# Weighted values and second expert layers on four 32-column TensorE tiles, with other shares for the chains

## Chip, cores and metric

The kernel runs on one core of a Trainium2 chip. The metric is the device time in microseconds of one execution; the time before is the median of three runs.

## What is computed

One layer of a vision transformer over 16 images, each cut into 1024 patches of 768 numbers. Cut to what matters:

```python
h = patches @ W.T + b                            # 1024 tokens of 256
q, k, v = split(layernorm(h) @ w_qkv)            # 8 heads of 32
k = sum over f = 1..256 of a[f]*sin(f*k) + b[f]*cos(f*k)
attn = softmax(q @ k.T * scale)                  # 1024 x 1024 for each head
h = h + (attn @ v) @ w_out + b_out
n = layernorm(h)
shared = relu(relu(n @ sW1) @ sW2) @ sW3
expert[e] = relu(relu(n @ eW1[e]) @ eW2[e]) @ eW3[e]     # 4 experts, 256-128-64-256
h = h + shared + sum over the best 2 of 4 experts, weighted by their gates
```

All arithmetic is in float32, some matmuls in its float32r form.

## The kernel before

The work is laid out in 130 *rounds* (`rd`). A round holds the transform of keys for half a pair of heads and the attention of one *attention unit* `att`: a pair of heads against 512 queries. There are 128 units (4 pairs, 2 blocks of queries, 16 images), and attention runs two rounds behind the transform.

In the **transform**, integer angles are loaded from DRAM as tiles `w` (L898), or spread from `src` into `f` (L938). GpSimd multiplies them by a frequency (L953) and ScalarE takes sines (L963). `mix(g)` multiplies by coefficients into a PSUM tile `kan` (L987): 64 rows by 32 columns, eight tiles of the array at once. VectorE multiplies `kan` by the fast sines (L1001), and `add_up(q)` sums the products over the waves into `red` (L1020): 128 rows by 32 columns, four tiles at once. These are the sums over waves.

In **attention**, `score(att, kc)` forms 128 keys by 512 queries for both heads of the pair on the full array (`sT`, L1085); `exponential` takes exp on ScalarE into `es` (L1100, three buffers). `weigh(att, kc)` multiplies `es` by the values and accumulates over the eight blocks `kc` into one PSUM tile `av` (L1117). The tile `v` holds, for each pair, 32 columns of values of the first head, 32 of ones, and 32 of values of the second. Two matmuls of 64 columns each therefore give values and denominator of head 0, then denominator and values of head 1:

```python
for s in range(2):
    nc.tensor.matmul(
        out=acc[0][ts(s, 64), :],
        lhsT=v[:, kc, p % NPAIR, ds(HD * s, 64)],
        rhs=es[:, ts(s, 512)], ...
```

`normalize(att)` then takes reciprocals (L1143), multiplies into `aT` (L1150), and adds a check (L1162), on VectorE.

All the rest is **chains**, four generators that yield pieces of work: chain 0 makes keys, queries and values, chain 1 projections (`proj`), gates and networks (`s1p`, `e1p`, `s2p`, `e2p`, `e3p`, `wb`, `wT`), chain 2 the rest of the gate weights, and chain 3 tokens (`tok`) and first norms (`lnT`). In `networks`, `second_of_experts` does the second layer of two experts in one PSUM tile `e2p`, again with two matmuls of 64 columns.

The order on every engine is written out by a **planner** before the kernel is built. The fixed steps of PE, ACT and the others lie in queues by `put`; `run` lays for PE either the next fixed step or a piece of a chain. It keeps a clock per engine and adds `SWITCH` when a step's tiling (`TILINGS`, for the kinds `mix`, `av`, `red`) differs from that of the last. A fixed step in the tiling that PE is in is preferred to a piece that would change it. `PACES` gives for each chain a share: for each unit of time of fixed work on PE its debt `due` grows by the share, up to a most. A chain in debt may go ahead of a fixed step. `now["stream"]` sums the columns streamed, from which the cost of a piece follows. SP's queue issues the loads and stores; it also takes its place in this plan.

The gate's matmuls (L727) are 128 rows by 32 columns too and carry the tiling of `red`.

Of the kernel before, what the change touches and what calls it, by code (L numbers as in the profile page):

```python
# [20 lines left out]
NPAIR = 4  # L21
HD = 32
N = 1024
NT = N // P
# [29 lines left out]


LAG, LANDS, TABLE, PER_COLUMN, SWITCH, IDLE = 0.06, 2.0, 1.28, 1.0 / 600, 0.18, 0.3
PACES = ((0.155, 2), (0.44, 2), (0, 0), (0.178, 2.6))

TILINGS = {"mix": (64, 32), "av": (128, 64), "red": (128, 32)}

@with_exitstack
def plain_path(ctx: ExitStack, tc: tile.TileContext, a: dict, out: bass.AP, verdict: bass.AP):
# [9 lines left out]
    nc = tc.nc  # L72
# [58 lines left out]
    w2e = load([P, NE, 64], a["eW2"].rearrange("e p f -> p e f"), "w2e")  # L131
# [7 lines left out]
    for i in range(4):  # L139
        nc.scalar.dma_start(out=biases[ds((NE + 1) * i, NE), 0, :], in_=a["eb3"])  # L140
        nc.scalar.dma_start(
            out=biases[ds((NE + 1) * i + NE, 1), 0, :], in_=a["sb3"].unsqueeze(0)
# [54 lines left out]
    v = const.tile([P, NT, NPAIR, 96], FP, tag="v", name="v")  # L197
# [24 lines left out]
    now = {"chain": 0, "stream": 0, "table": None, "dma": 0.0, "tiling": None, "piece": None}  # L222
# [38 lines left out]
    def matmul(out, lhsT, rhs, start, stop):  # L261
        now["stream"] += max(rhs.shape[-1], P)
        nc.tensor.matmul(out=out, lhsT=lhsT, rhs=rhs, start=start, stop=stop)  # L263
# [490 lines left out]
    def networks(b, half, late=False):  # L754

        if not late:
            yield from hold("networks")
        hT = images[b]["hT", half]
        w5 = fp.tile([P, 1024], FPR, tag="f", name="w5")[0:NW5, 0:512] if late else w5_

        def room(pool, n, name):
            return late_tile(n, name) if late else pool.tile([P, n], FP, tag=name[:2], name=name)

        def hidden(lhsT, name):
            ps = side_tile(name)
            for c in range(2):
                matmul(
                    out=ps,
                    lhsT=lhsT(c),
                    rhs=hT[:, c, :],  # L770
                    start=(c == 0),
                    stop=(c == 1),
                )
            return ps

        def first_of_expert(e):
            yield GO
            ps = hidden(lambda c: w1e[:, 2 * e + c, :], "e1p")
            yield ACT, 0.6
            e1 = room(ff2, 512, "e1")  # L780
            nc.scalar.activation(e1, ps, AF.Relu, bias=b1e[:, e : e + 1])
            return e1

        def second_of_experts(u, e1):
            yield GO
            ps = side_tile("e2p")
            now["piece"] = TILINGS["av"]
            now["stream"] -= 512
            for s in range(2):
                matmul(  # L790
                    out=ps[ts(s, 64), :],
                    lhsT=w2e[:, 2 * u + s, :],
                    rhs=e1[s],
                    start=True,
                    stop=True,
                )
            yield ACT, 0.6
            t = room(ff2, 512, "e2")
            nc.scalar.activation(t, ps, AF.Relu, bias=b2e[:, u : u + 1])  # L799
            return t  # L800

        def weigh_experts(u, t):
            yield GO
            wb = side_tile("wb")
            now["stream"] -= 300
            matmul(out=wb, lhsT=sel[:, u, :], rhs=w5, start=True, stop=True)
            yield DVE, 0.63
            nc.vector.tensor_mul(t, wb, t)

        if not late:  # L810
            yield from hold("s1")
        s1 = room(ffp, 1024, "s1").rearrange("p (m n) -> p m n", m=2)
        for m in range(2):
            yield GO
            ps = hidden(lambda c, m=m: w1s[:, c, ts(m, P)], "s1p")
            yield ACT, 0.6
            nc.scalar.activation(s1[:, m, :], ps, AF.Relu, bias=b1s[:, m : m + 1])
        e1 = [(yield from first_of_expert(0))]
        yield GO
        ps = side_tile("s2p")  # L820
        for c in range(2):
            matmul(
                out=ps,
                lhsT=w2s[:, c, :],
                rhs=s1[:, c, :],
                start=(c == 0),
                stop=(c == 1),
            )
        if not late:
            locks.remove("s1")  # L830
        yield ACT, 0.6
        s2 = room(ffp, 512, "s2")
        nc.scalar.activation(s2, ps, AF.Relu, bias=b2s)
        e1.append((yield from first_of_expert(1)))
        yield lambda: "bands" not in locks
        chains[now["chain"]]["ready"] = max(ch["ready"] for ch in (chains[now["chain"]], chains[2]))
        yield GO
        ps = side_tile("wT")
        for t in range(4):
            transpose(  # L840
                ps[0:NW5, ts(t, P)],
                bands.bitcast(FP)[:, t, :, :].rearrange("p i e -> p (i e)"),
            )
        locks.remove("gates")
        yield ACT, 0.48
        nc.scalar.copy(w5, ps[0:NW5, :])
        e2 = [(yield from second_of_experts(0, e1))]
        e1 = [(yield from first_of_expert(2))]
        yield from weigh_experts(0, e2[0])
        e1.append((yield from first_of_expert(3)))  # L850
        e2.append((yield from second_of_experts(1, e1)))
        yield from weigh_experts(1, e2[1])
        h = images[b]["h", half]
        for pr in range(2):
            yield GO
            ps = side_tile("e3p").rearrange("p (t e) -> p t e", e=E)
            parts = ((s2, w3s), (e2[0], w3e[:, 0, :]), (e2[1], w3e[:, 1, :]), (w5, b3))
            for t in range(2):
                for i in range(4):
                    lhsT, rhs = parts[3 - i if t else i]  # L860
                    matmul(
                        out=ps[:, t, :],
                        lhsT=lhsT[:, ts(2 * pr + t, P)],
                        rhs=rhs,
                        start=(i == 0),
                        stop=(i == 3),
                    )
            yield DVE, 0.63
            hh = h[:, ds(2 * pr, 2), :]
            nc.vector.tensor_add(hh, ps, hh)  # L870
        nc.sync.dma_start(
            out=out[b, ts(half, 512), :].rearrange("(t p) e -> p t e", p=P), in_=h
        )
        done["written", b, half] = sent(1.6, 0.5)
        if not late:
            locks.remove("networks")
# [231 lines left out]
    def weigh(att, kc):  # L1108

        p = att // 2  # L1110

        def action():
            if kc == 0:
                acc[0] = avp.tile([P, 512], FP, tag="av", name="av")
            es = exps.pop(kc)
            for s in range(2):
                nc.tensor.matmul(  # L1117
                    out=acc[0][ts(s, 64), :],
                    lhsT=v[:, kc, p % NPAIR, ds(HD * s, 64)],
                    rhs=es[:, ts(s, 512)],  # L1120
                    start=(kc == 0),
                    stop=(kc == NT - 1),
                )

        deps = [("exp", att, kc)]
        if kc == 0:
            b, i = divmod(p, NPAIR)
            deps.append(("all values" if i == NPAIR - 1 else "values", b))
            if att > 0:
                deps.append(("norm", att - 1))  # L1130
        put(PE, "fixed", 0.86, deps, ("av", att, kc), action)
# [84 lines left out]
    for rd in range(B * RI + 2):  # L1216
        groups = range(GS * rd, min(GS * rd + GS, total))
        att = rd - 2
        attends = 0 <= att < ATT
        for g in groups[::2]:  # L1220
            first = g == groups[0]
            for i, j in ((0, 0), (0, 1), (1, 0), (1, 1), (0, 2), (1, 2)):
                sine(g + i, j, TABLE if first and i == j == 0 else 0.0)
            mix(g)
            mix(g + 1)
        if groups:
            add_up(groups[0] // 2)

        def table():
            now["table"] = AF.Exp  # L1230
            nc.scalar.activation(spare[:, 1:2], spare[:, 0:1], AF.Exp)  # L1231

        put(ACT, "fixed", TABLE + 0.2, [], ("table", rd), table)
        for n in range(0, NT + 2, 2):
            if attends and n < NT:
                for kc in (n, n + 1):
                    score(att, kc)
                    exponential(att, kc)
            if n == 2 and groups:
                add_up(groups[0] // 2 + 1)  # L1240
            if attends and n > 0:
                for kc in (n - 2, n - 1):
                    weigh(att, kc)
    with tc.manual_schedule():
        run()

# [746 lines left out]
```

## Time and profile before

| | |
|---|---|
| median of 3 runs | 4168.1 us (4166.77 to 4168.17) |
| profiled execution | 4171.0 us, span 4169.3 us, clock 0.993 |
| PE matmuls | 22753, busy 4027.4 us |
| weight loads | 22753, busy 1766.4 us |
| av (L1117) | 4096 matmuls, busy 965.1 us |
| sT (L1085) | 2048, 691.7 us |
| kan (L987) | 8192, 623.9 us |
| red (L1020) | 2048, 273.6 us |
| e2p | 256, 69.1 us |
| ACT, POOL, DVE busy | 3286.3, 3195.8, 2830.2 us |
| DMA queue of SP | 906.98 MB, 78.7% of 16 engines |

A row of a timeline gives the start of a run of like instructions, its length, the engine, the line and operation, the tiles out<-in, then for matmuls the rows and columns of the array used, the shape and the count; a bracket holds the idle time before it and what ended it. A float32 matmul of the program stands as two instructions, a float32r one (`sT`, for example) as one. "PEld" is the loading of weights, which overlaps matmuls. The ends of matmuls are modelled, so the differences between starts are the better measure.

### The profile page before, as it was taken

To read this page: it belongs to the slowest core of one execution; us is meant where nothing else is said; L and a number is where in the kernel's file an instruction comes from. 1 tells how busy PE (TensorE), PEld (TensorE's weight loads), DVE (VectorE), ACT (ScalarE), POOL (GpSimd) and SP (SyncE) were. 2 spreads that over 40 slices of the span, in tenths; PEclk is the share of its full clock that TensorE was granted. 3 is DMA by queue.
4 is the path that set the end of the run, shared out by engine and by line. 5 is a ranking of instruction groups with operands and counts; after the bars stand their busy time and mean duration, and the time that the engine had idled before them with its cause. 6 is when DMAs were issued, how large, how long until landed. Compare 5 with 4: busy or idle time off the path is not lost.

```text
span 4169.3 us, 67564 instructions
## 1 busy us (share of the span) xinstructions
PE 4027.4 (97%) x22753; PEld 1766.4 (42%) x22753; DVE 2830.2 (68%) x4172; ACT 3286.3 (79%) x3939; POOL 3195.8 (77%) x2323
## 2 busy tenths in 40 slices
PE   6889999999999999999999999999999999999998
PEld 4324344443434445344444444444444444443334
DVE  4667767677676776767767677776767767677652
ACT  2688888788787888878788888788788788888873
POOL 3988877778787887878787787888778787787850
PEclk9999999999999999999999999999999999999999
DMA  7988878888787887978878878887887978878740
GB/s 223 263 241 222 243 200 223 238 218 247 207 232 219 239 235 210 244 211 224 247 209 238 221 225 225 228 241 209 234 228 219 251 211 239 219 211 226 197 138 16
DMA packets 587478, 914.27 MB, mean 219 GB/s; under 512 B 58828, under 2 KB 177524, under 8 KB 587124
## 3 DMA queue, kind: packets, MB, share of 16 engines
q1 hardware_dynamic: 580880, 906.98, 78.7%
q8 instruction: 184, 3.01, 0.3%
q10 hardware_dynamic: 6244, 2.88, 0.3%
q14 instruction: 170, 1.39, 0.1%
HBM read 758.64 MB, written 150.99 MB: 218 GB/s over the span
## 4 chain that ended last, share of the span: by engine, by line
PE 74%; ACT 10%; DVE 6%; DMA 5%; issue 3%; SPq 2%; POOL 1%; ACTq 0%; DVEq 0%; POOLq 0%
PE av L1117 18%; PE sT L1085 11%; PE kan L987 9%; PE tok L263 6%; PE e3p L263 5%; PE red L1020 5%; PE e1p L263 5%; ACT w L963 4%; DMA w<-ud 3%; PE s1p L263 3%; PE q L263 2%; PE v L263 2%; PE proj L263 2%; DVE f L1001 2%; PE k L263 2%
## 5 line engine op out<-in xcount | busy, mean ns | idle before, releaser
L953 POOL TENSOR_TENSOR w<-w,lane 128x1024 int32<-128x1024 int32 x1024 | 1926.1, 1896 | 444.4 <-DMA w<-ud 298.6
L1100 ACT ACTIVATE es<-sT 128x1024 f32<-128x1024 f32 x1024 | 1033.0, 1022 | 550.0 <-PE av L1117 339.8
L953 POOL TENSOR_TENSOR f<-f,lane 128x1024 int32<-128x1024 int32 x512 | 971.0, 1896 | 251.2 <-DVE f L938 157.5
L963 ACT ACTIVATE w<-w 128x1024 f32<-128x1024 int32 x1024 | 1021.1, 1048 | 42.1 <-POOL w L953 39.1
L1117 PE MATMUL av<-es,v 128*64 128x512 f32 x4096 | 965.1, 602 | 1.0 <-DVE rc L1162 1.0
L1143 DVE RECIPROCAL rc<-av 128x256 f32<-128x256 f32 x256 | 434.0, 1730 | 702.6 <-PE av L1117 702.6
L1085 PE MATMUL sT<-q,k 128*128 128x512 f32 x2048 | 691.7, 449 | 42.0 <-DVE f L1001 20.2
L1001 DVE TENSOR_TENSOR f<-kan,f 128x1024 f32<-128x1024 f32 x512 | 608.5, 1218 | 159.8 <-ACT f L963 123.7
L938 DVE STREAM_SHUFFLE f<-src 128x1024 int32<-128x1024 int32 x512 | 673.0, 1353 | 0.7
L987 PE MATMUL kan<-w,coef 64*32 64x512 f32 x8192 | 623.9, 600 | 39.5 <-ACT w L963 35.6
L1085 PEld LDWEIGHTS sT<-q,k 128*128 128x128 f32 x2048 | 346.0, 189 | 440.5 <-issue 219.0
L963 ACT ACTIVATE f<-f 128x1024 f32<-128x1024 int32 x512 | 516.1, 1048 | 2.6 <-POOL f L953 2.6
L1117 PEld LDWEIGHTS av<-es,v 128*64 128x64 f32 x4096 | 258.5, 136 | 563.2 <-issue 498.2
L263 PE MATMUL tok<-wt,x 128*128 128x256 f32 x1536 | 362.3, 387 | 16.9 <-DMA w1s<-in_sW 13.6
L263 PEld LDWEIGHTS tok<-wt,x 128*128 128x128 f32 x1536 | 288.7, 192 | 110.8 <-issue 34.7
L987 PEld LDWEIGHTS kan<-w,coef 64*32 64x32 f32 x8192 | 127.9, 105 | 375.2 <-ACT w L963 222.5
L1020 PE MATMUL red<-f,pack 128*32 128x512 f32 x2048 | 273.6, 604 | 1.5 <-DVE f L1001 1.3
L263 PE MATMUL e1p<-hT,w1e 128*128 128x512 f32 x480 | 233.2, 608 | 0.4 <-ACT e L799 0.4
L462 ACT ACTIVATE hn<-h,less,rstd 128x256 f32<-128x256 f32 x256 | 143.8, 591 | 51.6 <-POOL less L454 51.2
L963 ACT ACT_TABLE_LOAD x128 | 164.2, 1283 | 22.4 <-DMA w<-ud 20.2
L1150 DVE TENSOR_TENSOR aT<-av,rc 32x512 f32<-32x512 f32 x256 | 176.1, 688 | 6.4
L1231 ACT ACT_TABLE_LOAD x128 | 164.2, 1283 | 2.2
(125 smaller groups left out, 3746.7 us busy)
## 6 DMA issues: line engine op xcount, KB each, us to landing
w<-ud SPq DMA_DIRECT2D x2048, 256.0 KB
q<-qd SPq DMA_DIRECT2D x512, 128.0 KB
k<-kd SPq DMA_DIRECT2D x128, 512.0 KB
x<-in_xT SPq DMA_DIRECT2D x128, 384.0 KB
ud<-u SPq DMA_DIRECT2D x64, 512.0 KB
ud<-ui SPq DMA_DIRECT2D x64, 512.0 KB
src<-ud SPq DMA_DIRECT2D x512, 64.0 KB
qd<-qhi SPq DMA_DIRECT2D x64, 256.0 KB
```

The lines of the kernel that those rows point to most:

```text
L263: nc.tensor.matmul(out=out, lhsT=lhsT, rhs=rhs, start=start, stop=stop)
L938: nc.vector.stream_shuffle(w, sources[g // 8].rearrange("p r n -> p (r n)"), [4 * (g % 8) + i // 8 for i in range(32)],)
L953: nc.gpsimd.tensor_tensor(w, w, f.to_broadcast([P, N]), ALU.mult)
L963: nc.scalar.activation(x, w, AF.Sin, scale=TURN * 2.0**-32)
L987: nc.tensor.matmul(out=ps[ds(64 * j + 32 * blk, 32), ts(r, 512)], lhsT=coef[ts(r, 64)].rearrange("p e f j -> p (e f j)"), rhs=w[ts(r, 64), ...
L1001: nc.vector.tensor_mul(w, kan.pop(g), w)
L1020: nc.tensor.matmul(out=rows_of_pair[p][ts(2 * i + r, 32), :], lhsT=pack[:, ds(PACK0 - 16 * (k % 2) - 2 * (k // 2), 32)], rhs=prod[:, ts(r, ...
L1085: nc.tensor.matmul(out=ps[:, ts(s, 512)], lhsT=k4[:, 2 * s + kc // 4, ts(kc % 4, P)], rhs=q4[:, s, :], start=True, stop=True,)
L1100: nc.scalar.activation(es, scores.pop(kc), AF.Exp, scale=SCALE)
L1117: nc.tensor.matmul(out=acc[0][ts(s, 64), :], lhsT=v[:, kc, p % NPAIR, ds(HD * s, 64)], rhs=es[:, ts(s, 512)], start=(kc == 0), stop=(kc == ...
L1143: nc.vector.reciprocal(rc[0][:, part], acc[0][:, part])
L1150: nc.vector.tensor_mul(aT[ds(64 * (i % 2) + HD * s, HD), i // 2, ts(qb, 512)], acc[0][ds(96 * s, HD), :], rc[0][ds(HD + HD * s, HD), :],)
```

## The change

The matmuls of `weigh` and of `second_of_experts` are written as four of 32 columns in place of two of 64. The two tiles of one head stream the same columns of `es` (or the same `e1`). The planner's entry `"av"` becomes (128, 32), which is that of `"red"`, so that it sees no change between these kinds. `PACES` gets other shares, and a smaller most for chain 3. The planner's count of columns for `e2p` is 512 before and after. The loop that laid the attention steps is replaced by a string: s is a score with its exponential, r the second sum over waves of the round, w a weighing.

```diff
-PACES = ((0.155, 2), (0.44, 2), (0, 0), (0.178, 2.6))
-
-TILINGS = {"mix": (64, 32), "av": (128, 64), "red": (128, 32)}
+PACES = ((0.2, 2), (0.48, 2), (0, 0), (0.16, 2))
+
+TILINGS = {"mix": (64, 32), "av": (128, 32), "red": (128, 32)}
+ATTENTION = "ssssrwwsswwsswwww"
...
             now["piece"] = TILINGS["av"]
-            now["stream"] -= 512
-            for s in range(2):
-                matmul(
-                    out=ps[ts(s, 64), :],
-                    lhsT=w2e[:, 2 * u + s, :],
-                    rhs=e1[s],
+            now["stream"] += 512
+            for i in range(4):
+                nc.tensor.matmul(
+                    out=ps[ts(i, 32), :],
+                    lhsT=w2e[:, 2 * u + i // 2, ts(i % 2, 32)],
+                    rhs=e1[i // 2],
...
-            for s in range(2):
+            for i in range(4):
                 nc.tensor.matmul(
-                    out=acc[0][ts(s, 64), :],
-                    lhsT=v[:, kc, p % NPAIR, ds(HD * s, 64)],
-                    rhs=es[:, ts(s, 512)],
+                    out=acc[0][ts(i, HD), :],
+                    lhsT=v[:, kc, p % NPAIR, ds(HD * (i - i // 2), HD)],
+                    rhs=es[:, ts(i // 2, 512)],
...
-        for n in range(0, NT + 2, 2):
-            if attends and n < NT:
-                for kc in (n, n + 1):
-                    score(att, kc)
-                    exponential(att, kc)
-            if n == 2 and groups:
-                add_up(groups[0] // 2 + 1)
-            if attends and n > 0:
-                for kc in (n - 2, n - 1):
-                    weigh(att, kc)
+        scored, weighed = iter(range(NT)), iter(range(NT))
+        sums = iter(range(groups[0] // 2 + 1, groups[-1] // 2 + 1) if groups else ())
+        for kind in ATTENTION:
+            if kind == "r" and groups:
+                add_up(next(sums))
+            elif kind == "s" and attends:
+                kc = next(scored)
+                score(att, kc)
+                exponential(att, kc)
+            elif kind == "w" and attends:
+                weigh(att, next(weighed))
```

## The prediction

> **What bounds the kernel now.** I read the page first: its engine shares, its slices and its chain.
>
> ```profile
> PE 4027.4 (97%) x22753; PEld 1766.4 (42%) x22753; DVE 2830.2 (68%) x4172; ACT 3286.3 (79%) x3939; POOL 3195.8 (77%) x2323
> ...
> PE   6889999999999999999999999999999999999998
> ...
> PE 74%; ACT 10%; DVE 6%; DMA 5%; issue 3%; SPq 2%; POOL 1%; ACTq 0%; DVEq 0%; POOLq 0%
> PE av L1117 18%; PE sT L1085 11%; PE kan L987 9%; PE tok L263 6%; PE e3p L263 5%; PE red L1020 5%; PE e1p L263 5%; ACT w L963 4%; DMA w<-ud 3%; PE s1p L263 3%; PE q L263 2%; PE v L263 2%; PE proj L263 2%; DVE f L1001 2%; PE k L263 2%
> ```
>
> TensorE is the bound, except in the first three slices. The busy time by windows sharpens this:
>
> ```profile
> 105.00:490.00 385.00, 349.98 (x1971) 133.50 (x1972) 256.71 (x362) 306.05 (x348) 335.10 (x208) 0.98 0.89 241
> 490.00:2040.00 1550.00, 1529.52 (x8823) 679.75 (x8820) 1092.81 (x1606) 1269.80 (x1522) 1229.71 (x885) 1.00 0.83 227
> 2040.00:3830.00 1790.00, 1767.23 (x10138) 780.14 (x10140) 1268.10 (x1857) 1467.81 (x1766) 1425.05 (x1035) 1.00 0.82 227
> ```
>
> The columns are the window, its length, then busy time of PE, PEld, DVE, ACT and POOL, the granted clock, DMA share and GB/s. From 490 to 3830 us PE idles 20.5 + 22.8 = 43.3 us of 3340, while ACT is busy 82%. So a microsecond of work taken from PE there is nearly a microsecond of time.
>
> But busy time hides what PE loses when its array is cut into other tiles. The timeline of PE shows it, if one subtracts the start of a run from the start of the next:
>
> ```profile
> 1512.35 1.06 PE L1020 MATMUL red<-f,pack 128*32 128x512 f32 x8
> 1513.34 1.94 PE L1117 MATMUL av<-es,v 128*64 128x512 f32 x8
> 1515.21 1.19 PE L1085 MATMUL sT<-q,k 128*128 128x512 f32 x4
> ...
> 1519.33 3.65 PE L1117 MATMUL av<-es,v 128*64 128x512 f32 x16
> 1522.91 1.98 PE L263 MATMUL q<-hnT,wq 128*128 128x512 f32 x4
> 1524.73 2.75 PE L263 MATMUL tok<-wt,x 128*128 128x256 f32 x12
> 1527.41 1.95 PE L987 MATMUL kan<-w,coef 64*32 64x512 f32 x32
> 1529.29 0.66 PE L267 MATMUL lnT<-ident,hn 128*128 128x128 f32 x4
> ...
> 1533.53 0.64 PE L727 MATMUL gate<-hT,gw 128*32 128x128 f32 x16
> 1534.11 1.98 PE L263 MATMUL q<-hnT,wq 128*128 128x512 f32 x4
> 1535.93 0.27 PE L267 MATMUL gateT<-ident,rows 128*128 128x128 f32 x1
> ```
>
> An f32 matmul stands as two instructions, and matmuls on disjoint tiles stream together. So av x8 is two tiles by four passes, x16 eight passes, red x8 four tiles by two passes, kan x32 eight tiles by four passes. **A pass** costs (3.65 - 1.94)/4 = 0.43 us. **A run between two changes of tiling costs its passes and a fixed part**, which is:
> - av: 1515.21 - 1513.34 = 1.87, less 4 x 0.429, leaves 0.15 us; the x16 run gives 3.58 less 8 x 0.429, again 0.15.
> - red: 0.99 less 2 x 0.429 leaves 0.135.
> - kan: 1.88 less 4 x 0.429 leaves 0.164.
> - full array: q between gate and gateT shows the entry, 1.82 less 4 x 0.429 = 0.10; tok before kan shows the exit, 2.68 less 12 x 0.216 = 0.09 (0.216 from unbroken 256-column runs); together 0.195.
>
> **What the Trainium skill says.** "TensorEngine Tiling (Array Packing)", Tiling Modes, Key Properties, states that changing the mode, not merely the tile, drains TensorE. The fixed parts above agree and price it. "TensorE: Matmul & The Clock Gate", section LDWEIGHTS, says that a load scales with its columns. The means of the weight loads agree in direction: 189 ns for 128 columns (sT), 136 for 64 (av), 108 for 32 (red), though they are not proportional. The same page, Part 3, says that matmuls on separate column groups run at the same time, each further tile adding about 4 ns. The second point I use below as the reason why av's entry gets no dearer.
>
> **The change part by part.**
>
> *The tile width.* av and e2p go from two tiles of 64 to four of 32. The passes stay: 1024 av steps and 64 e2p steps of two passes each, and four tiles stream at once. The trace shows that this width sustains the rate when passes follow each other:
>
> ```profile
> 133.53 1.92 PE L1020 MATMUL red<-f,pack 128*32 128x512 f32 x16
> ```
>
> x16 is four passes, and (1.92 - 1.06)/2 = 0.43 us for each added one. New are 2,048 + 128 program matmuls, twice that in traced instructions and in weight loads (22753 becomes about 27,100). A kan run issues sixteen matmuls and sixteen loads in a step of the same length, more than the eight and eight that av will have, so issue is not the limit. The instruction queues carried 4.4 of 914 MB; I cost a few tenths of a MB more at nothing.
>
> *The changes of tiling.* av, e2p, red and gate now have one tiling, so neighbours among them form one run. I counted runs in the built instruction orders of both programs, on the path that executes:
>
> - 128x64: 433 before, 0 after
> - 128x32: 319 before, 597 after
> - 64x32 (kan): 349 before, 313 after
> - full array: 833 before, 803 after
> - 32 rows: 128 in both
>
> In 109 of 128 rounds red stood directly ahead of av; now in 126, and there a whole change vanishes. Before: 433 x 0.151 + 319 x 0.135 + 349 x 0.164 + 833 x 0.195 = 65.4 + 43.1 + 57.2 + 162.4 = 328.1 us. After: 597 x 0.135 + 313 x 0.164 + 803 x 0.195 = 80.6 + 51.3 + 156.6 = 288.5 us. **The difference is -40 us.** All of it lies on PE.
>
> *The string of the attention steps* spells ssss r ww ss ww ss wwww, which is the order that the loop laid before: 0 us.
>
> *The shares of the chains (PACES)* move the pieces of other work (tokens, norms, keys, networks) among the fixed steps. The counts of instructions on ACT, DVE, POOL and SP stay the same, table loads included; only their places move, and SP's loads and stores with them. Per round of 32 us, the side work on PE (passes by price) was 6.5 to 18.3 us in the first cycle of eight rounds that repeats (rounds 31 to 63 of 130), and is 9.3 to 20.1 in the new one (30 to 117). A round with little of it could be set by others. How short a round they allow shows early, where PE has almost no side work and waits for ACT's sines:
>
> ```profile
> 239.64 3.90 PE L987 MATMUL kan<-w,coef 64*32 64x512 f32 x32 [1.78 <-ACT w L963]
> ...
> 265.69 3.90 PE L987 MATMUL kan<-w,coef 64*32 64x512 f32 x32 [1.78 <-ACT w L963]
> ```
>
> That is 26.05 us from round to round. With passes and fixed parts the leanest of the new steady rounds still holds about 27.2 us of PE work, so it covers ACT, POOL and the loads of waves, with little to spare. I put new waiting at 0 and bound it by -10 and +25 us: the middle idles 43 us now, and a half more than that would be +22. In some seven early rounds PE isn't the bound, and the change saved there, 7 x 0.15, is lost: +1.
>
> *The end.* After the last av both halves are projected, and PE waits:
>
> ```profile
> 4086.56 3.72 PE L263 MATMUL proj<-wo,aT 128*128 128x256 f32 x16
> 4090.65 0.70 PE L263 MATMUL proj<-wo,aT 128*128 128x256 f32 x2 [0.36 <-DVE h L706]
> 4092.07 3.33 PE L263 MATMUL proj<-wo,aT 128*128 128x256 f32 x14 [0.72 <-DVE aT L1150]
> 4098.86 2.80 PE L267 MATMUL lnT<-ident,hn 128*128 128x128 f32 x8 [3.46 <-ACT hn L462]
> ```
>
> In the new order the first half's projection stands between the last scores, and its transposes and gate fill the time in which DVE normalizes. Late next is the second half's aT, for some 2 us. Of 0.36 + 0.72 + 3.46 = 4.5 us I count -2 to -3.
>
> No wait is added: an av step waits for its es as before, and ACT's exponentials, queued behind the release of es by av, see that release no later.
>
> **Sum.** -40 + 0 + 1 - 2.5 = -41.5 us against the profiled execution's own 4171.0 us (span 4169.3 and 1.7 around it), so 4129.5. The median shown, 4168.1, is 2.9 lower; the same sum from it is about 4127. I take 4128.
>
> **Rivals.**
>
> 1. *Narrow tiles stream worse (slower).* If the four weight loads of a pass are not hidden in av, where two tiles read the same es columns at once, each pass pays what the first pass of a red run pays: 0.135 less an exit of 0.09 and some 0.02 of further tiles, so about 0.025 us. With 2 x (1024 + 64) = 2176 passes that is +54, net +13: about 4181. It decides from 40/2176 = 18 ns a pass on. The x16 run of red speaks against it; for it speaks only that red's four tiles never shared a moving operand.
> 2. *Half the gain is lost to waiting.* The uneven rounds run into ACT, POOL (298.6 us of waits for w by the list of waits) or DMA (0.82 busy). With +20: 4148. For it: 27.2 against 26.05 us is a thin margin, and a round's own pieces load ACT too. Against it: the order of before had rounds as lean.
> 3. *The new placement also removes waits in the middle.* Ten of its 43 us gone: 4118.
>
> **How the numbers follow.** Forecast 0.68, rival 2 0.17, rival 3 0.09, rival 1 0.06. The range of 4110 to 4154 takes the forecast with both bounds of the waiting, and rivals 2 and 3. A measurement here can tell about 0.2%, 8 us. Faster by more is the forecast, rival 3 and nearly all of rival 2: 0.92. The rest of rival 2 and the mild half of rival 1 are the same: 0.04; slower 0.04.
>
> **What would show it.** In the timeline after: red and av as one stretch, the av start 0.86 us after red's instead of 0.99; av x16 where x8 stood, still four passes in 1.72 us plus about 0.135 at the exit; 27,100 matmuls. PE's busy time near 3990 us and its share still 96 to 97%. Wrong would be: passes over 0.43 us (rival 1), or PE idling over 60 us between 490 and the last 340 us with releases from ACT or DMA (rival 2).

## The result and the profile after

The changed kernel takes **4149.0 us** (median of 4 runs, 4144.04 to 4151.49) against 4168.0 for the kernel before in the same comparison: ratio 0.9954, 95% interval 0.9936 to 0.9971. A repetition with the experiments gave 4147.5 and 0.9948 (0.9935 to 0.9960). That is faster by 19 to 21 us where the forecast had 40: the sign held, about half of the gain is missing, and the time is that of rival 2.

The page's lines on engines, on the chain that ended last (shares by engine) and on the group of av:

```profile
PE 3994.8 (96%) x27105; PEld 1747.8 (42%) x27105; DVE 2817.9 (68%) x4172; ACT 3285.3 (79%) x3939; POOL 3193.0 (77%) x2323
...
PE 65%; ACT 14%; DMA 7%; DVE 6%; issue 4%; SPq 3%; POOL 1%; ACTq 0%; DVEq 0%; POOLq 0%
...
L1118 PE MATMUL av<-es,v 128*32 128x512 f32 x8192 | 956.7, 596 | 2.2 <-DVE rc L1163 2.2
```

PE's work, 27105 matmuls and 3995 us busy, is as predicted. The chain tells of the rest: PE's share fell from 74 to 65%, ACT's rose from 10 to 14%. The busy time by windows of the same two stretches as before:

```profile
490.00:2040.00 1550.00, 1526.63 (x10562) 680.44 (x10556) 1095.78 (x1622) 1276.30 (x1531) 1236.61 (x901) 1.00 0.83 228
2040.00:3830.00 1790.00, 1764.21 (x12157) 776.73 (x12150) 1263.63 (x1855) 1476.90 (x1771) 1432.42 (x1029) 1.00 0.83 227
```

PE now idles 23.4 + 25.8 = 49.2 us there, before 43.3. That looks harmless, and it misled: much waiting stands inside the runs that the page calls busy, as shown below. The timeline of PE at a steady spot answers the lines on tilings:

```profile
2876.10 1.07 PE L1021 MATMUL red<-f,pack 128*32 128x512 f32 x8
2876.99 1.90 PE L1118 MATMUL av<-es,v 128*32 128x512 f32 x16
2878.82 1.49 PE L1086 MATMUL sT<-q,k 128*128 128x512 f32 x4
```

av starts 0.89 us after red here (0.88 in all 126 such places: two passes of 0.43 and some 0.02), and its four passes and exit take 1.83.

**Where the time went.** I counted PE's work in the built order of each program (passes and fixed parts as in the prediction, entries and exits priced apart) and took it from the time between starts in the trace; what is left is called *loss*.

The count has one fault: it prices the transposes of 128 columns (lnT, wT) at twice their time, for eight of lnT take 1.07 us from start to start, 0.11 each when the change of tiling is taken off (timeline of the stretch with keys, below). So work stands some 70 us too high in every kernel, and up to 0.9 us in a stretch that holds them; the differences between kernels hardly move.

In the two profiled executions (4171.0 and 4144.0 us) the work fell from 3937 to 3898 us, -39; the loss in rounds 0 to 29 rose by 3.7, in rounds 30 to 117 by 14.5, and fell by 9 at the end; +1 before the first score and +2 after the last matmul. Sum: -27, which is their difference. The medians differ by only 19, since before's profile lies 3 us above its median and after's 5 below.

A part of what counts as loss is the clock. In both profiles there are windows of 3.4 us, or two or three in a row, in which PE was granted half its clock (0.50 as granted clock). From the first score to the last matmul before's profile has 27.3 us of such time and after's 3.4, which is worth up to half of it, 13.7 and 1.7 us: up to 12 of the 27 us between the two profiles. Most of it, 20.5 us against 3.4, lies in the last rounds.

To place the loss, I cut a round in two. The **T stretch** goes from the last weighing of a unit to the first score of the next; it holds the mixes, the first sum and pieces of chains. The **A stretch** goes from first score to last weighing. In attention rounds 30 to 115, 86 of each kind (us; the price of the transposes makes some sums negative). The last column is half of the time at half clock there, the most that the loss of that row can owe to the clock:

| kernel | PE work in T | T under 13 us of work: number, loss | other T: loss | A under 14: number, loss | other A: loss | clock, at most |
|---|---|---|---|---|---|---|
| before | 1260 | 17, 25.0 | -13.1 | 8, 9.8 | 23.8 | 3.4 |
| after | 1186 | 22, 38.7 | -1.2 | 0 | 23.1 | 0 |
| e1_tiles_only | 1259 | 17, 25.7 | -11.4 | 8, 9.9 | 22.7 | 0 |
| e2_tiles_tiling | 1231 | 21, 52.9 | 13.2 | 18, 36.5 | 28.9 | 11.9 |
| e3_paces_only | 1202 | 32, 32.8 | -4.3 | 11, 28.1 | 21.3 | 5.1 |
| e4_tiles_paces | 1202 | 32, 33.3 | -2.4 | 11, 29.0 | 29.9 | 5.1 |
| e7_paces_c1 | 1280 | 0 | 3.4 | 21, 55.1 | 25.7 | 13.7 |
| e8_paces_c2 | 1222 | 18, 31.8 | 6.4 | 10, 16.6 | 33.1 | 6.8 |
| e9_v1 | 1220 | 33, 22.2 | -8.7 | 0 | 48.6 | 13.7 |
| e10_v2 | 1261 | 22, 22.5 | -12.5 | 0 | 32.0 | 0 |
| e13_relu_dve | 1186 | 22, 33.3 | -7.4 | 0 | 24.4 | 1.7 |
| e14_short_keys | 1186 | 22, 29.2 | -1.2 | 0 | 25.5 | 0 |

The change carried 74 us of PE work out of the T stretches; short ones became more, and lose more. With the transposes at 0.11 us each, and a first score that follows another full-array matmul counted from the end of that matmul, the same stretches give +15 us in lean T stretches, +9 in fuller ones and -11 in A stretches, so the picture stands.

### The profile page after: what moved, and what is told of

Same layout as the page of the kernel before. It is cut to its first block, busy times and chain, and to the rows that moved or that the text cites. A ratio compares the mean times of both kernels' runs of the same rounds, so it can differ in the third digit from the quotient of the medians.

```text
span 4142.4 us, 76256 instructions
## 1 busy us (share of the span) xinstructions
PE 3994.8 (96%) x27105; PEld 1747.8 (42%) x27105; DVE 2817.9 (68%) x4172; ACT 3285.3 (79%) x3939; POOL 3193.0 (77%) x2323
## 4 chain that ended last, share of the span: by engine, by line
PE 65%; ACT 14%; DMA 7%; DVE 6%; issue 4%; SPq 3%; POOL 1%; ACTq 0%; DVEq 0%; POOLq 0%
PE av L1118 15%; PE sT L1086 10%; PE kan L988 7%; ACT w L964 6%; PE tok L264 6%; PE red L1021 5%; PE e1p L264 4%; PE proj L264 3%; ACT f L964 3%; DMA w<-ud 3%; PE s1p L264 3%; PE k L264 3%; SPq L918 2%; PE q L264 2%; DVE f L1002 2%
## 5 line engine op out<-in xcount | busy, mean ns | idle before, releaser
L1118 PE MATMUL av<-es,v 128*32 128x512 f32 x8192 | 956.7, 596 | 2.2 <-DVE rc L1163 2.2
L1086 PE MATMUL sT<-q,k 128*128 128x512 f32 x2048 | 692.9, 450 | 43.3 <-DVE f L1002 24.2
L1118 PEld LDWEIGHTS av<-es,v 128*32 128x32 f32 x8192 | 239.7, 109 | 551.3 <-issue 491.2
L964 ACT ACT_TABLE_LOAD x128 | 164.2, 1283 | 22.2 <-DMA w<-ud 19.9
L463 ACT ACTIVATE hn<-h,less,rstd 128x256 f32<-128x256 f32 x256 | 144.1, 594 | 37.8 <-POOL less L455 37.7
L1232 ACT ACT_TABLE_LOAD x128 | 164.2, 1283 | 2.3
```

The lines of the kernel that those rows point to most:

```text
L964: nc.scalar.activation(x, w, AF.Sin, scale=TURN * 2.0**-32)
L1086: nc.tensor.matmul(out=ps[:, ts(s, 512)], lhsT=k4[:, 2 * s + kc // 4, ts(kc % 4, P)], rhs=q4[:, s, :], start=True, stop=True,)
L1118: nc.tensor.matmul(out=acc[0][ts(i, HD), :], lhsT=v[:, kc, p % NPAIR, ds(HD * (i - i // 2), HD)], rhs=es[:, ts(i // 2, 512)], start=(kc == 0),
```

## The experiments

In the expectations, "Theory A" is that PE's work fell as forecast and that the new order of pieces brings waits, because some stretches hold so little PE work that other engines set their length. Its rivals are that the tiles themselves cost, or that PE's work alone decides. "Floor" is the length under which a round or stretch does not go, "evenness" that side work is spread evenly over rounds. PACES are (share, most) for the chains 0 to 3; the changed kernel has (0.2, 2), (0.48, 2), (0, 0), (0.16, 2).

### Which part brings the loss

**The tiles alone.** The changed kernel with

```diff
-PACES = ((0.2, 2), (0.48, 2), (0, 0), (0.16, 2))
-TILINGS = {"mix": (64, 32), "av": (128, 32), "red": (128, 32)}
+PACES = ((0.155, 2), (0.44, 2), (0, 0), (0.178, 2.6))
+TILINGS = {"mix": (64, 32), "av": (128, 64), "red": (128, 32)}
```

so that the orders are those of before.

> Tile width alone: the matmuls of av and e2p on four tiles of 32, but the planner's entry for av and PACES as before, so that every engine's order is that of the kernel before. By the fixed parts of the runs (433 entries 27 ns cheaper, exits 13 ns dearer, 109 red-av and 14 gate-av changes of about 0.15 us gone) PE has 26 us less. Theory A (the seams are priced right, and what was lost in the changed kernel is waiting that its new order brings): the waits stand where they stood, so nearly all of it is gained, about 4142 to 4146. Theory B (other engines close behind PE take back about half of whatever is taken off PE in the middle, in any order): about 4155.

Measured: 4151.5, ratio 0.9962 (0.9949 to 0.9975). Work 3911 us, -26; the stretches lose what they lost before (46.9 us in the four columns, 45.5 before). Narrow tiles lengthen no pass, and some 17 us arrive (10 to 21 by the interval). That lies between the two theories, 4142 to 4146 and 4155; where the other 9 us stay isn't known.

**Tiles and the planner's tiling, old PACES:**

```diff
-PACES = ((0.2, 2), (0.48, 2), (0, 0), (0.16, 2))
+PACES = ((0.155, 2), (0.44, 2), (0, 0), (0.178, 2.6))
```

> The changed kernel with the old PACES: four tiles, and the planner told of them. PE work by the same count is 37 us less than before, but in its steady cycle the PE work of a round runs from 19.6 to 39.2 us. Theory A: a round of 19.6 us can't be shorter than the 26 us that the other engines need, 6 us lost in each of some 11 cycles: 4168 - 37 + 20 to 60, so no gain, 4150 to 4190. Theory B: half of 37, about 4150.

Measured: 4224.4, ratio 1.0130 (1.0115 to 1.0144), with 3900 us of PE work: 37 us less work, 56 us more time, beyond both theories. Up to 12 us of that is half clock (table).

**Tiles and new PACES, old tiling in the planner:**

```diff
-TILINGS = {"mix": (64, 32), "av": (128, 32), "red": (128, 32)}
+TILINGS = {"mix": (64, 32), "av": (128, 64), "red": (128, 32)}
```

> Four tiles and the new PACES, but the planner's entry for av still (128, 64). PE work by count 36.6 us less than before, 2.3 more than the changed kernel; rounds of 25.8 to 35.3 us, more even than its 27.2 to 37.1. Theory A: waits as in an even order, about 4168 - 36 + 5 = 4137, faster than the changed kernel. Theory B: 4150, like the changed kernel.

Measured: 4177.9, ratio 1.0022 (1.0013 to 1.0032): a miss. Work is 3901, but short stretches of both kinds lose 62 us. The evenness of whole rounds is not what decides.

**New PACES alone,** the kernel before with

```diff
-PACES = ((0.155, 2), (0.44, 2), (0, 0), (0.178, 2.6))
+PACES = ((0.2, 2), (0.48, 2), (0, 0), (0.16, 2))
```

> The kernel before with the new PACES alone: tiles of 64, planner's entry (128, 64). PE work by count 3929, 8 us less than before; stretches between weighings and scores hold 1366 us in place of 1441 and lack 81 in place of 51, and from scores to weighings 20 in place of 11. Theory A: 4168 - 8 + 40, about 4200; the same order on four tiles took 4178, and four tiles alone gained 17 to 22 in the old order. Work alone: 4160.

Measured: 4186.3, ratio 1.0055 (1.0041 to 1.0069). That lies between the two expected times. So new shares cost 19 us with wide tiles (e3) and 26 with narrow ones (e4 against e1) under the old tiling, and the new tiling 73 us under the old shares; together they take nothing from e1's gain and add little to it. The repetition of the changed kernel belongs to this group:

> The changed kernel again, beside the others: 4144 to 4151. Its four runs spread over 7.4 us where the kernel before spread over 1.4; the profile shows whether the extra time of a slower run lies in a few rounds or in all.

Measured: 4147.5, as told above.

### Is it the lean stretches?

Eight rounds repeat in the changed kernel. Two of the eight T stretches are lean: one with keys, 11.6 us of PE work by the count in 13.6, and one with experts, 12.0 in 13.5. With the transposes at 0.11 us they hold 10.7 and 11.7 and lose 3.0 and 1.8 each round; two fuller ones, with 14.1 us of work, lose 1.7 (keys) and 0.9 (experts). Two mixes were made twice in these (e5) or in two fuller ones (e6), 37.8 us of added PE work in either; the result is not changed by it.

```diff
-            for j in range(2):
+            twice = 32 <= g // GS < 120 and g // GS % 8 in (3, 5) and g % GS < 2
+            for _ in range(2 if twice else 1):
+                for j in range(2):
...
```

(e6 has `in (4, 7)`.)

> The changed kernel; in 22 middle rounds (3 and 5 of every 8) the first two mixes of the round are issued twice, with the same result. That is 22 x 2 x 2 passes of 0.429 us = 37.8 us more PE work, placed where PE has the least to do between the last weighing of one unit and the first score of the next: 11.6 and 12.0 us. Theory A (that stretch has a floor of its own, about 14 us, set by ScalarE's table load and twelve sines; what a round lacks there is lost): nearly free, +0 to +8 us on the changed kernel, so 4148 to 4156. Theory B (PE is the bound all through, and what was lost has another cause): +38, about 4186.

> The same 37.8 us of repeated mixes in 22 other rounds (4 and 7 of every 8), whose stretch before the first score already holds 14.7 us of PE work. Both theories: +33 to +40 on the changed kernel, about 4184; the pair with the kernel before it tells.

Measured: e5 4168.1, ratio 0.9992 (0.9984 to 1.0000); e6 4183.8, ratio 1.0029 (1.0018 to 1.0040). Against 4147.5 the same work costs 21 us in the lean stretches and 36 in the full ones (18 and 34 by the ratios, as before was slower beside these two runs). Between e5 and e6, which ran together, lie 15.7 us: that much disappears in waits that were there. This is shown, but e5 lies between its two expected times: the lean stretches grew from 13.6 to 14.5 and from 13.5 to 14.7 us, so they have no fixed length of 14.

### Other shares

```diff
 e7:  PACES = ((0.215, 2), (0.44, 2), (0, 0), (0.18, 2))
 e8:  PACES = ((0.2, 2), (0.44, 2), (0, 0), (0.18, 2))
 e9:  PACES = ((0.21, 2), (0.47, 1.5), (0, 0), (0.178, 2)), ATTENTION = "sssswwrsswwsswwww"
 e10: PACES = ((0.2, 2.6), (0.49, 1.5), (0, 0), (0.178, 1.5))
```

> The changed kernel with PACES 0.215, 0.44, 0, 0.18, picked from the built order: PE work by count as in the changed kernel (3899 against 3898), but the stretches between weighings and scores of the middle rounds (98 of them) hold 1450 us in place of 1355, so that with a floor of 14 us they lack 16 in place of 66 us; the stretches from first score to last weighing lack more (44 against 8). Theory A: 13 us under the changed kernel, about 4135. Theory B, by work alone: the same as the changed kernel, 4148.

> The changed kernel with PACES 0.2, 0.44, 0, 0.18: PE work by count 3886.5, 12 us less than the changed kernel, lacking 56 us between weighings and scores and 22 from scores to weighings. Theory A: 3964.7 by work and lacks against 3972.4, about 4140. Theory B, by work alone: 4136.

Measured: e7 4182.3, ratio 1.0025 (1.0017 to 1.0033), e8 4174.7, ratio 1.0008 (0.9999 to 1.0016): two misses. e7 cured the lean T stretches, but 21 A stretches became short and lose 55 us. PE's and ACT's timelines of one of them (12.5 us of work in 17.2):

```profile
2924.99 0.73 PE L1086 MATMUL sT<-q,k 128*128 128x512 f32 x2 [0.34 <-DVE f L1002]
2927.04 0.74 PE L1086 MATMUL sT<-q,k 128*128 128x512 f32 x2 [1.32 <-ACT es L1101]
2928.44 1.06 PE L1086 MATMUL sT<-q,k 128*128 128x512 f32 x2 [0.67 <-ACT es L1101]
```

```profile
2925.99 1.00 ACT L1101 ACTIVATE es<-sT 128x1024 f32<-128x1024 f32 x1
2926.89 0.59 ACT L463 ACTIVATE hn<-h,less,rstd 128x256 f32<-128x256 f32 x1
2927.38 1.01 ACT L1101 ACTIVATE es<-sT 128x1024 f32<-128x1024 f32 x1
```

With nothing laid between the scores, they follow each other at the pace of the exponentials, and a norm (`hn`) behind each makes that 1.4 us. That was read, not tried, and it isn't the whole loss: right after these waits PE ran at half clock. The same instructions here and in the one of the last seven such stretches (one in eight rounds) that kept its full clock:

```profile
2929.44 1.94 PE L1021 MATMUL red<-f,pack 128*32 128x512 f32 x8
2931.14 2.35 PE L1118 MATMUL av<-es,v 128*32 128x512 f32 x16
...
3436.55 1.07 PE L1021 MATMUL red<-f,pack 128*32 128x512 f32 x8
3437.43 1.90 PE L1118 MATMUL av<-es,v 128*32 128x512 f32 x16
```

```profile
2928.70:2932.10 3.40, 3.40 (x18) 0.77 (x21) 3.40 (x6) 1.09 (x2) 3.16 (x10) 0.51 0.91 239
3435.90:3439.30 3.40, 3.40 (x27) 0.99 (x27) 3.40 (x6) 2.03 (x3) 3.16 (x10) 1.00 0.82 228
```

red takes 1.70 us from start to start in place of 0.88, and the stretch 17.2 in place of 15.6. e8 has the least PE work of all, 3886 us, and is no faster than before: PE's work alone does not decide the time.

> The changed kernel with PACES 0.21 (most 2), 0.47 (most 1.5), 0, 0.178 (most 2), and the second sum over waves of a round after the first two weighings (ssss ww r ss ww ss wwww). PE work by count 3898, as in the changed kernel; rounds of the middle 25.4 to 33.5 us. Between weighings and scores the middle holds 1393 us (1355 in the changed kernel), but unevenly, 82 us below a floor of 14 (66). Theory A with that floor: 4148 + 9, some 4157. If rather the evenness of whole rounds decides (33.5 at most in place of 37.1): under 4140.

> The changed kernel with PACES 0.2 (most 2.6), 0.49 (most 1.5), 0, 0.178 (most 1.5), the string unchanged. PE work by count 3898.3, the same as in the changed kernel to 0.1 us, so any difference is waiting. Between weighings and scores the middle holds 1439 us, as in the kernel before (1441), and lacks 52 us below a floor of 14 in place of 66; the stretches from scores to weighings lack 4 in place of 8. Theory A: 19 us under the changed kernel, about 4130. Work alone: 4148.

Measured: e9 4131.5, ratio 0.9907 (0.9893 to 0.9920), a miss of the floor: stretches of 12.0 to 12.4 us lost nothing there, while the one with keys took 13.6 us as in the changed kernel. So the floor is not one number; it depends on which pieces the stretch holds. e9's executions ran from 4120 us at a mean granted clock of 0.995 to 4139 at 0.992; the slowest is the profiled one, and up to 13.7 of its 48.6 us of loss in the A stretches is half clock. e10: **4127.4, ratio 0.9906** (0.9890 to 0.9921), as expected. Its PE work is that of the changed kernel, 3898 us; it has as much of it in the T stretches as before (1261 us). The whole forecast gain, 40 us, is there with other shares.

### What sets the length of a lean stretch

PE's timeline of the stretch with keys, in the changed kernel:

```profile
2883.22 3.64 PE L1118 MATMUL av<-es,v 128*32 128x512 f32 x32
2886.79 1.09 PE L268 MATMUL lnT<-ident,hn 128*128 128x128 f32 x8
2887.86 1.06 PE L988 MATMUL kan<-w,coef 64*32 64x512 f32 x8
2889.29 1.06 PE L988 MATMUL kan<-w,coef 64*32 64x512 f32 x8 [0.37 <-ACT w L964]
2890.29 1.98 PE L264 MATMUL k<-hnT,wk 128*128 128x512 f32 x4
...
2896.01 2.40 PE L988 MATMUL kan<-w,coef 64*32 64x512 f32 x32
2898.34 1.07 PE L1021 MATMUL red<-f,pack 128*32 128x512 f32 x8
2900.42 0.73 PE L1086 MATMUL sT<-q,k 128*128 128x512 f32 x2 [1.01 <-DVE f L1002]
```

The idle times sum to 1.4 us; the kan run of 32, four passes and a change of 1.9 us elsewhere, lasts 2.3 from start to start, so it too waited inside. The first mix stands in two halves with a wait for a sine between, and takes 2.4 us up to k where 1.0 is enough for x16. The score is the first that needs the PSUM tile of `kan`, which the product f frees. ACT in the same window has not a gap (one table load, twelve sines, two copies, 13.75 us; its first and last lines):

```profile
2885.46 1.28 ACT L964 ACT_TABLE_LOAD   x1
2886.75 1.06 ACT L964 ACTIVATE w<-w 128x1024 f32<-128x1024 int32 x1
2887.72 0.57 ACT L472 COPY hnT<-lnT 128x512 f32<-128x512 f32 x1
2888.18 1.06 ACT L964 ACTIVATE w<-w 128x1024 f32<-128x1024 int32 x1
2889.14 0.58 ACT L472 COPY hnT<-lnT 128x512 f32<-128x512 f32 x1
...
2893.40 3.89 ACT L964 ACTIVATE w<-w 128x1024 f32<-128x1024 int32 x4
2897.19 2.00 ACT L964 ACTIVATE f<-f 128x1024 f32<-128x1024 int32 x2
2899.21 1.28 ACT L1232 ACT_TABLE_LOAD   x1
```

The table load agrees with the Trainium skill, "ScalarE activation tables: per-element evaluation and per-set limits", What a function is on this engine, which puts two functions in different sets 1283 ns apart. I took ACT for what binds, and moved the two copies (`hnT`, L472; also `hT`) to DVE:

```diff
-            nc.scalar.copy(dst[:, c, :], ps)
+            nc.vector.tensor_copy(dst[:, c, :], ps)
```

> The changed kernel with one line changed: the copy of hnT out of PSUM is made by DVE instead of ACT, so that ACT's chain in the stretch from last weighing to first score loses its copies of 0.57 us (two in each lean stretch) and PE's work and order stay as in the changed kernel. Theory A (ACT's unbroken run of one table load, twelve sines and two copies, 13.75 us, sets how short that stretch can be): the lean stretches that wait now get up to 1.1 us shorter each, 8 to 15 us in all, 4134 to 4141, and the loss in these stretches falls from 37.5 to under 28 us. Rival (DVE, which has the product of the sines to make and then the copies too, or PE's own order sets it): 4148 or slower, the loss as it was.

Measured: 4188.9, ratio 1.0041 (1.0027 to 1.0054). The stretch with keys grew from 13.6 to 14.5 us, another A stretch from 20.3 to 21.1; the one with experts stayed. The A stretch after the keys grew too, from 17.4 us to between 18.7 and 19.4 in nine of eleven rounds, but this is the clock: those nine have a window at half clock, and the other two took 17.4 as in the changed kernel. One of the nine, and one of the two:

```profile
2932.29 4.39 PE L264 MATMUL tok<-wt,x 128*128 128x256 f32 x12
2936.33 0.81 PE L1086 MATMUL sT<-q,k 128*128 128x512 f32 x2
...
2177.49 2.75 PE L264 MATMUL tok<-wt,x 128*128 128x256 f32 x12
2179.89 0.82 PE L1086 MATMUL sT<-q,k 128*128 128x512 f32 x2
```

The twelve matmuls of tok take 4.0 us to the next start in place of 2.4. So of the 40 us that e11 lost, some 10 are the stretch with keys, 9 the other A stretch, and 15 half clock. The theory that ACT alone binds fell, since the stretch with keys grew. DVE, in the same window of the changed kernel, has no gap either:

```profile
2886.93 3.37 DVE L1144 RECIPROCAL rc<-av 128x256 f32<-128x256 f32 x2 [7.07 <-PE av L1118]
...
2892.31 0.69 DVE L538 TENSOR_SCALAR turns<-k 128x512 int32<-128x512 f32 x1
2893.10 0.70 DVE L539 SCALAR_TENSOR_TENSOR k<-turns,k 128x512 f32<-128x512 int32 x1
2893.71 2.35 DVE L1002 TENSOR_TENSOR f<-kan,f 128x1024 f32<-128x1024 f32 x2
2895.97 1.42 DVE L543 SCALAR_TENSOR_TENSOR k<-turns,k 128x512 f32<-128x512 int32 x2
...
2899.15 2.35 DVE L1002 TENSOR_TENSOR f<-kan,f 128x1024 f32<-128x1024 f32 x2
```

It works from the reciprocals to the product, 2899.15, that the score waits for. Two runs took work from one engine each. The first leaves out the reciprocals of the second 256 queries:

```diff
-                nc.vector.reciprocal(rc[0][:, part], acc[0][:, part])
+                nc.vector.tensor_copy(rc[0][:, part], rc[0][:, ts(0, 256)]) if half else nc.vector.reciprocal(rc[0][:, part], acc[0][:, part])
```

> The changed kernel with the second of the two reciprocals of a unit replaced by a copy of the first half's result (left out: the reciprocals of the second 256 queries); every order stays. DVE's work right after the last weighing shrinks by some 1.3 us, ACT's and PE's do not change. Two-chain theory: in the lean stretch with keys (11.6 us of PE work, 13.6 us long, once in eight rounds) DVE runs without a break from the reciprocals to the product that frees kan's PSUM, so that stretch gets 0.9 us shorter, until ACT's last sines bind; the lean stretch with experts (12.0 us of work, 13.5 long), in which DVE waits for ACT, stays. In all 10 to 14 us: 4134 to 4138, loss in the stretches 37.5 to about 27. ACT-alone theory: no change, 4148, both stretches as before.

Measured: 4149.6, ratio 0.9953 (0.9939 to 0.9967): no change, both stretches as before; the expectation missed. DVE's timeline says why:

```profile
2893.87 0.69 DVE L538 TENSOR_SCALAR turns<-k 128x512 int32<-128x512 f32 x1 [1.09 <-PE k L264]
```

The time won is spent waiting for k. DVE's reciprocals are not on the path; what follows k is. The second run moves the rectifier of an expert's first layer from ACT to DVE:

```diff
-            nc.scalar.activation(e1, ps, AF.Relu, bias=b1e[:, e : e + 1])
+            nc.vector.tensor_scalar(out=e1, in0=ps, scalar1=b1e[:, e : e + 1], scalar2=0.0, op0=ALU.add, op1=ALU.max)
```

> The changed kernel with the rectifier of an expert's first layer (e from e1p) made by DVE in place of ACT, 0.66 us each; every order stays. Two-chain theory: the lean stretch with experts (12.0 us of PE work, 13.5 long, ACT without a break for 14.4 us, DVE idle 1.1 us) holds one such piece and gets 0.4 to 0.7 us shorter; the lean stretch with keys, which holds none, stays at 13.6. In all about -7 us: 4141, unless DVE, heavier elsewhere by 0.7 us, holds up a score. DVE-alone theory: the stretch with experts stays or grows by 0.7, 4148 to 4160.

Measured: 4141.7, ratio 0.9938 (0.9924 to 0.9951), -6 us on the changed kernel, whose interval overlaps this one, and -8 on e12, which ran beside it. The stretch with experts went from 13.48 to 12.96 us, one fuller one (14.5 us of work) from 14.59 to 14.03, the one with keys stayed: in the stretches with experts ACT does bind. By the table that is 12 us in the T stretches; more than the medians show, and the granted clock was lower here (0.993 in the median run, 0.995 in e12's). Then k's own work, with two correction steps of its range reduction left out:

```diff
-            for part in (TWO_PI_B, TWO_PI_C):
+            for part in ():
```

> The changed kernel with the two small correction steps of the keys' range reduction left out (k in place, 0.71 us each on DVE); every order stays. Keys-path theory: in the lean stretch with keys (11.6 us of PE work, 13.6 long) the path runs through k on PE, then DVE's passes over k and the products of the sines in one unbroken queue, to the first score; shorter by 1.4 us on DVE, the stretch shrinks by 0.9 us until ACT's last sines bind: 11 such stretches in the middle, some 8 to 11 us in all, 4136 to 4140, the stretch with experts unchanged at 13.5. ACT theory (the sines alone set it): 4148, 13.6 stays.

Measured: 4133.2, ratio 0.9910 (0.9893 to 0.9926). The stretch with keys went from 13.61 to 12.74 us, the one with experts stayed. DVE now waits for ACT before the product, so that ACT's sines are the next bound, 0.9 us further down:

```profile
2890.89 2.36 DVE L1002 TENSOR_TENSOR f<-kan,f 128x1024 f32<-128x1024 f32 x2 [0.37 <-ACT f L964]
```

So the end of that stretch's path is shown: k on PE, then DVE's passes over k laid ahead of the product, then the first score. What sets k's start is read from the timelines and not tried: k starts right where the second half of the first mix ends, 2890.29, and that half waited for ACT's second sine, which follows the table load, one sine and a copy. The copies themselves ended 0.6 us before k started. The eleven stretches account for 9.6 us of the 14 between the medians; the two profiles, 4144.0 and 4134.2, differ by 9.9.

Last, the two edits that keep the result and helped, e10 with the rectifier on DVE:

> e10_v2 (the changed kernel with the shares (0.2, 2.6), (0.49, 1.5), 0, (0.178, 1.5)) with the rectifier of an expert's first layer made by DVE in place of ACT, as in e13_relu_dve. Its lean stretches lose only 10 us, so less is to be had there than the 6 us of e13: in the waits of wb and e2p for ACT (13 us together) some 3 to 6 us, 4121 to 4125. If DVE's added 0.7 us a piece hold up scores instead: 4127 or above.

Measured: 4127.4, ratio 0.9897 (0.9881 to 0.9914). The intervals of e10 and e15 overlap, so no further gain is shown there; the 4121 to 4125 that I expected did not come.

## Why the prediction was right in sign and wrong in size

**Right: the tile width and the changes of tiling.** Passes stayed at 0.429 us, red and av became one stretch, and PE's work fell by 39 us for a forecast 40. The place between red and av also fits "TensorEngine Tiling (Array Packing)", Key Properties, of the Trainium skill: no change of mode, no drain, 0.88 us for two passes. Rival 1 is refuted by the passes and by e1, which is faster where rival 1 is slower. But of the 26 us that e1 takes off PE only 17 arrived, so a microsecond of PE's work was not quite a microsecond of time even in the old order.

**Wrong: the step "the shares of the chains", with new waiting put at 0.** I tested the leanest new round, 27.2 us of PE work, against the 26.05 us of an early round. But a round is not free to use its PE work anywhere. Its first score waits for a product of sines, and a T stretch with 11.6 us of PE work by the count waits 2 us (3 with the transposes at 0.11) though an A stretch of 17.4 follows in the same round. The floor had to be tested on each of the two stretches, with the pieces that stand in it. The early round could not show that: its own T stretch took some 11.7 us (from 259.0 to the first score at 270.73), but it held no keys or experts to lengthen DVE's and ACT's part. In place of 0 came +14.5 us in rounds 30 to 117 (up to 18 without the half clock in before's profile), within the bound of 25 but beyond the value taken. By the table it is +13.7 in the lean T stretches and -9.8 in short A stretches that vanished; some 11 us lie in fuller T stretches, in the main in the two with keys and experts (e13 takes 6 of them back).

**Terms that were mis-sized.** Rounds 0 to 29: +3.7 and +1 for the opening, forecast +1. The end: -9 in the last rounds, +2 after the last matmul, forecast -2.5. Up to 8.5 of the -9 is half clock. Half of those 20.5 us in before's profile, 10.2, began at 4098.5, just as PE had stood idle for 3.46 us; whether the change took them away or chance did is open. Without the half clock the last rounds lose about the same before and after. That these terms nearly cancel in the sum is luck.

**The sum against the median.** The profiles differ by 27 us and the medians by 19. The spread goes with the clock: among 84 executions of the kernel before, those with a mean granted clock of 0.992 took 4174.1 us on average, those with 0.995 took 4166.5. The profile of before (0.993) stands on the slow side, that of after (0.996) on the fast one, so the pair flatters the change.

**Rival 2** named the mechanism and its number, 4148, though not DVE, which binds in the stretch with keys. Its sign was too coarse, over 60 us of idle PE, where 49 were found: a run of like instructions that waits inside counts as busy. Its reason against, "the order of before had rounds as lean", holds for rounds; before had 17 lean T stretches, after 22.

## What to carry to other kernels

When an edit moves side work, cut the period at every point where another engine must hand something over, count the bound engine's work in each piece and hold it against the chains of the other engines there, with the pieces that actually stand in it; the whole period says little. A saving counts only in pieces that stay above that floor. The shares and the planner's tiling belong together: the same narrow tiles gave 4224, 4178, 4148 or 4127 us with nearly the same PE work. And before a longer stretch is put down to an engine, look at the granted clock in it.

## What the runs showed of the hardware that I had not expected

A wait can hide in a busy figure: the kan run above is listed with 2.40 us where the same 32 instructions take 1.95 elsewhere. And an engine without a gap need not bind: ACT (13.75 us unbroken) and DVE both ran full through the stretch with keys, yet taking 1.1 us from ACT made it longer, since DVE got the work, and taking 1.2 us from DVE ahead of k changed nothing; of the DVE work tried, only that behind k counted.

A wait can also be followed by half clock. Where the score behind the stretch with keys found PE idle for 1.0 us (the changed kernel), none of eleven rounds had a window at half clock; where it found PE idle for 2.0 us (e11), nine of eleven had one, which cost up to 2 us each. No run here tried what sets it off.
